# Mixture-of-experts kernel: 684 inner columns as five chunks of 128 and one shared remainder chunk

## The chip, the cores and the metric

The kernel runs on one core of a Trainium2 chip. Its time is the device time of one execution in microseconds (us). Three timed runs of the kernel before took 1914.9, 1920.45 and 1924.0 us; the median, 1920.45 us, is the time before. A profiled execution of its own took 1901.8 us; everything below that speaks of rows, waits and positions in time comes from that one execution.

The engines are named as the profile names them: PE is TensorE's matmul side and PEld its weight loading, DVE is VectorE, ACT is ScalarE, POOL is GpSimd and SP is SyncE, which here only issues DMAs.

## What is computed

The input is four sequences of 1024 tokens with 256 channels, all in float32. The layer is a transformer block with sandwich norms: attention with 16 heads of 16, then a mixture of eight experts of which each token uses two.

```python
def _moe_forward(x, centroid, Wg, bg, W1, b1, W2, b2):   # E = 8, K = 2, D = 256, H = 684
    ...
    w, sel = jax.lax.top_k(dist, K)          # the two farthest centroids
    w = jax.nn.softmax(w.astype(jnp.float32), axis=1).astype(x.dtype)
    ...
    for e in range(E):
        h = jax.nn.silu(xs @ Wg[e] + bg[e]) * (xs @ W1[e] + b1[e])
        out = out + we[:, e:e + 1] * (h @ W2[e] + b2[e])
    return out.reshape(x.shape)

x = x + _layernorm(_L0_attn_ref(_layernorm(x), ...))
x = x + _layernorm(_L0_ffn_ref(_layernorm(x), ...))
```

H = 684 is the number of inner columns of an expert. It is 6 x 114, and also 5 x 128 + 44.

## The kernel before

The kernel has three parts, one after the other on PE.

**Opening and attention, to about 1168 us.** The order of the instructions on PE, DVE and ACT is written out ahead by a planner. The function `step` emits the fixed work (scores `sc`, weighted values `av`, maxima `pm`), and between these it calls `run_one`, which takes the first piece of background work that fits. Background work is a generator wrapped in `Work`; before each of its pieces it yields the engines and nanoseconds that the piece is expected to take, such as `"P500 D400"`. The planner keeps a clock of its own from these numbers. A piece that starts on PE is let in when the planner's clock has passed the end of the piece before it; what a DMA takes is not in that clock unless the generator yields it as `W`. `late_constants` is one such generator. It is made with `Work(late_constants(), 40)`, where 40 is the step by which it is due and not a step before which it may not run. Each engine then executes its own instructions strictly in the order in which they were emitted.

SP's order is not written by hand in this part. SP issues, in this order: the loads that attention starts with; then 34 DMAs that write the tile `empty` over the whole DRAM buffer `rows` (the place where tokens are later scattered by expert); and the DMAs that lay the experts' weights and biases out in the DRAM buffer `wall`, one row of 128 partitions by `WW` floats for each expert. The first `wall` DMA comes ahead of the `rows` DMAs, all others behind them. On this queue at most eight DMAs are in flight: each waits for the one that was issued eight before it.

**The experts, about 1168 to 1829 us.** Tokens are sorted by expert into tiles of `TS` = 256 rows; there are `MT` = 39 tiles. A small table, computed on DVE from the counts per expert, gives each tile its expert and first row (`tabi`). For tile j, `fetch(j)` loads the tokens (`xt`) and the weights of the expert (`w`); `transposed` puts the tokens' channels on partitions (`px`, `xT`); `up` computes the inner columns, and `down` multiplies them by W2 and scatters the weighted rows into `res` with an indirect DMA on POOL. `up` works on chunks of `FP` = 114 inner columns, `NF` = 6 of them, each with four matmuls (two projections, two halves of the 256 channels). ACT takes silu of the gate projection out of PSUM (`sil`), DVE multiplies it by the other projection (`h`). `down` takes the six chunks for each half of the tile's tokens, i = 0 and 1; the last of the six has 115 rows, as a row of ones carries the bias b2. The order on SP, PE, DVE and ACT is written by hand: while tile j goes up, tile j - 1 goes down, and the tokens of tile j + 1 are transposed ahead of the last two chunks.

**The end, from 1829 us.** Results are gathered, normalised and stored. The change does not touch this part.

The line numbers are those of the profile. Lines that matter below: L191 `late_constants`; L226 the `rows` DMAs; L236 to L246 the `wall` DMAs; L1042 to L1069 the table; L1076 `fetch`; L1099 the transposes; L1114 the up-matmuls; L1133 the down-matmuls; L1159 the loads of `x` from `resid` that ACT issues at the start of the experts.

Of the kernel before, what the change touches and what calls it, by code (L numbers as in the profile page):

```python
# [8 lines left out]
F32 = mybir.dt.float32  # L9
# [30 lines left out]
O1, O2, OG, WW = KC * FF, 2 * KC * FF, 2 * KC * FF + NF * C, 2 * KC * FF + NF * C + 2 * NF  # L40
# [3 lines left out]
def sandwich(  # L44
# [168 lines left out]


# [18 lines left out]
    wall = tc.dram_tile([NE, P, WW], F32, name="wall")  # L233
    for e in range(NE):
        for i, w in enumerate((wg, w1)):
            nc.sync.dma_start(  # L236
                out=wall[e, :, i * O1 : (i + 1) * O1].rearrange("p (k f) -> p k f", k=KC),
                in_=w[e].rearrange("(k p) f -> p k f", p=P),
            )
        nc.sync.dma_start(  # L240
            out=wall[e, :FP, O2:OG].rearrange("p (f c) -> p f c", f=NF),
            in_=w2[e].rearrange("(f p) c -> p f c", p=FP),
        )
        nc.sync.dma_start(out=wall[e, FP : FP + 1, OG - C : OG], in_=b2[e : e + 1, :])
    for i, bias in enumerate((bg, b1)):
        nc.sync.dma_start(  # L246
            out=wall[:, :FP, OG + i * NF : OG + (i + 1) * NF].rearrange("e p f -> p e f"), in_=bias
        )
# [353 lines left out]
    def outputs(u, av):  # L602
# [32 lines left out]
        if g == NG - 1:  # L635
# [5 lines left out]
                after=[back] + [closing[k] for k in closing] + before_[:-1],  # L641
# [350 lines left out]
    with tc.manual_schedule(engines={ET.PE, ET.DVE, ET.Activation}):  # L992
# [17 lines left out]
        Work(late_constants(), 40)  # L1010
# [26 lines left out]

    pc = bank("counts")
    nc.tensor.matmul(pc[:, :NE], ones, seen, start=True, stop=True)
    one = slice(0, 1)  # L1040
    cnt = const.tile([1, NE], I32, tag="cnt", name="cnt")
    nc.vector.tensor_scalar(cnt, pc[one, :NE], float(TS - 1), None, ALU.add)  # L1042
    nc.vector.tensor_scalar(cnt, cnt, TS.bit_length() - 1, None, ALU.arith_shift_right)
    num = const.tile([1, NE], F32, tag="num", name="num")
    nc.vector.tensor_copy(num, cnt)
    tri = const.tile([1, NE, NE], F32, tag="tri", name="tri")
    nc.vector.tensor_tensor(
        tri, num[:, None, :].to_broadcast([1, NE, NE]), before[one], ALU.mult
    )
    first = const.tile([1, NE], F32, tag="first", name="first")  # L1050
    nc.vector.tensor_reduce(first, tri, AX.X, ALU.add)
    sh = [1, MT, NE]
# [20 lines left out]
    for h in hs:  # L1073
        nc.gpsimd.memset(h[96:P, NF - 1, :], 1.0)
# [116 lines left out]
    with tc.manual_schedule(engines={ET.SP, ET.PE, ET.DVE, ET.Activation}):  # L1191
        ready, last = [fetch(0), fetch(1)], None
        xT = transposed(0, ready[0][0])
        for j in range(MT):
            xt, w = ready.pop(0)
            up(j, w, xT, 0)
            for i in range(2):
                if last is not None:
                    down(*last, i)
# [95 lines left out]
```

## Time and profile before

| | before |
|---|---|
| median of three timed runs | 1920.45 us |
| profiled execution | 1901.8 us |
| its span, first to last instruction | 1900.0 us |
| PE busy | 1699.6 us (89%) |
| PE busy, 1220 to 1829 us | 608.6 of 609.0 us |
| DVE busy, whole span | 1067.6 us (56%) |
| mean granted PE clock | 0.946 |
| DMA traffic | 197 MB |

The page of a profile shows the span in 40 slices of 47.5 us each; a digit is the busy share in tenths, and 9 is 90% or more. `PEclk` is the clock that TensorE was granted, in tenths of full speed. In a row of instructions, `pu<-xT,w` means that the tile `pu` is written from `xT` and `w`; `128*114` is the shape that the weights take in the array and `128x256` that of the data that is streamed past them. In a timeline the first number is the start in us, the second the length of the merged piece, and `x32` the number of records in it. A line ends with the idle time of the engine just before, and with what ended it, where there was any. SPq and ACTq are the issuing of DMAs by these engines, and not the transfers.

### The profile page before, as it was taken

To read this page: it belongs to the slowest core of one execution; us is meant where nothing else is said; L and a number is where in the kernel's file an instruction comes from. 1 tells how busy PE (TensorE), PEld (TensorE's weight loads), DVE (VectorE), ACT (ScalarE), POOL (GpSimd) and SP (SyncE) were. 2 spreads that over 40 slices of the span, in tenths; PEclk is the share of its full clock that TensorE was granted. 3 is DMA by queue.
4 is the path that set the end of the run, shared out by engine and by line. 5 is a ranking of instruction groups with operands and counts; after the bars stand their busy time and mean duration, and the time that the engine had idled before them with its cause. 6 is when DMAs were issued, how large, how long until landed. Compare 5 with 4: busy or idle time off the path is not lost. (4 is left out here: it accounts for less than half of the span.)

```text
span 1900.0 us, 27442 instructions
## 1 busy us (share of the span) xinstructions
PE 1699.6 (89%) x9640; PEld 1068.7 (56%) x9640; DVE 1067.6 (56%) x2522; ACT 880.6 (46%) x1766; POOL 572.7 (30%) x1068
## 2 busy tenths in 40 slices
PE   4989999999999999999999992799999999999940
PEld 3444445544444454445444441688888888888840
DVE  6576687686677687676678844133333333333346
ACT  2357676776776676676575671111111111111113
POOL 5652422543471544542432132011111111111104
PEclk8899999999999999999999995799999999999975
DMA  8997500100000001000000001844444444444434
GB/s 251 301 299 207 142 1 12 34 34 12 23 1 23 24 34 34 1 12 23 1 35 18 29 31 36 274 167 163 165 162 163 163 164 167 163 164 166 167 125 155
DMA packets 101036, 196.99 MB, mean 104 GB/s; under 512 B 8094, under 2 KB 80437, under 8 KB 95907
## 3 DMA queue, kind: packets, MB, share of 16 engines
q1 hardware_dynamic: 83410, 160.65, 26.1%
q0 software_dynamic: 9040, 26.21, 4.1%
q10 hardware_dynamic: 8448, 8.39, 1.4%
q8 instruction: 76, 1.25, 0.3%
q14 instruction: 62, 0.50, 0.1%
HBM read 132.22 MB, written 79.86 MB: 112 GB/s over the span
## 5 line engine op out<-in xcount | busy, mean ns | idle before, releaser
L594 DVE TENSOR_REDUCE part<-pm 128x1 f32<-128x512 f32 x1024 | 647.6, 684 | 212.3 <-PE pm L590 209.2
L682 ACT ACTIVATE e<-sc 128x512 f32<-128x512 f32 x1024 | 538.2, 603 | 199.1 <-PE sc L678 191.4
L1114 PE MATMUL pu<-xT,w 128*114 128x256 f32 x1872 | 422.3, 383 | 7.4 <-DMA x<-resid 4.6
L1114 PEld LDWEIGHTS pu<-xT,w 128*114 128x114 f32 x1872 | 334.1, 180 | 77.1 <-issue 5.0
L1119 ACT ACTIVATE sil<-pu,w 114x256 f32<-114x256 f32 x234 | 110.3, 474 | 504.3 <-PE pu L1114 495.4
L1122 DVE SCALAR_TENSOR_TENSOR h<-pu,w,sil 114x256 f32<-114x256 f32 x234 | 112.9, 484 | 337.1 <-ACT sil L1119 337.0
L590 PE MATMUL pm<-stack,stack 64*128 64x512 f32 x960 | 267.9, 472 | 20.3 <-DVE part L594 15.5
L740 PE MATMUL av<-e,v 128*32 128x512 f32 x2048 | 281.7, 622 | 0.0
L1146 POOL DMA_INDIRECT res<-yo,ids x78 | 74.8, 959 | 567.8 <-DVE yo L1145 562.7
L671 PE MATMUL sc<-stack,stack 64*128 64x512 f32 x960 | 238.9, 439 | 1.3 <-ACT oT L766 0.7
L678 PE MATMUL sc<-shift,bring 64*128 64x512 f32 x1024 | 235.3, 407 | 3.7 <-ACT shift L579 3.5
L590 PEld LDWEIGHTS pm<-stack,stack 64*128 64x128 f32 x960 | 120.0, 188 | 200.8 <-DVE part L594 118.2
L1133 PE MATMUL pe<-w,h 114*128 114x256 f32 x936 | 214.9, 379 | 0.0
L1133 PEld LDWEIGHTS pe<-w,h 114*128 114x128 f32 x936 | 178.1, 190 | 25.1
L671 PEld LDWEIGHTS sc<-stack,stack 64*128 64x128 f32 x960 | 114.9, 187 | 64.1 <-issue 23.2
L678 PEld LDWEIGHTS sc<-shift,bring 64*128 64x128 f32 x1024 | 120.6, 190 | 25.8 <-ACT shift L579 14.2
L1145 DVE TENSOR_SCALAR yo<-pe,xt 128x256 f32<-128x256 f32 x78 | 37.7, 483 | 104.4 <-PE pe L1133 104.4
L538 ACT CAST stack<-ps 128x512 fp32r<-128x512 f32 x124 | 73.5, 595 | 49.3 <-PE ps L531 48.9
L531 PEld LDWEIGHTS ps<-ident_r,split 128*128 128x128 f32 x512 | 52.2, 144 | 64.3 <-POOL split L262 22.0
L531 PE MATMUL ps<-ident_r,split 128*128 128x128 f32 x512 | 69.4, 264 | 16.0 <-POOL split L262 15.9
L740 PEld LDWEIGHTS av<-e,v 128*32 128x32 f32 x2048 | 41.2, 109 | 72.6 <-issue 66.3
L929 POOL DMA_INDIRECT rows<-xr,to x64 | 62.7, 980 | 62.3 <-DVE to L924 44.7
(246 smaller groups left out, 1432.6 us busy)
## 6 DMA issues: line engine op xcount, KB each, us to landing
w<-wall SPq DMA_DIRECT2D x39, 1368.0 KB, 6.7
rows<-empty SPq DMA_DIRECT2D x34, 1032.0 KB, 15.5
w<-wall SPq DMA_DIRECT2D x39, 689.3 KB
wall<-in_w_dram SPq DMA_DIRECT2D x16, 684.0 KB
xt<-rows SPq DMA_DIRECT2D x39, 258.0 KB
wall<-in_wg_dram SPq DMA_DIRECT2D x8, 684.0 KB
xb<-in_x_dram POOLq DMA_DIRECT2D x8, 512.0 KB, 4.3
resid<-xb SPq DMA_DIRECT2D x8, 512.0 KB, 3.8
```

The lines of the kernel that those rows point to most:

```text
L531: nc.tensor.transpose(ps[:, t * P : (t + 1) * P], splits[b, g, half][:, t, is_k, 2 * pr : 2 * pr + 2].rearrange("p h n d -> p (h n d)"), i ...
L590: nc.tensor.matmul(pm, q[r, t * P : (t + 1) * P], k_[r, half * TB : (half + 1) * TB], start=True, stop=True,)
L594: nc.vector.tensor_reduce(part[:, i, 2 * pr + s, half : half + 1], pm, AX.X, ALU.max)
L671: nc.tensor.matmul(sc, k_[r, kb * P : (kb + 1) * P], q[r, qb * TB : (qb + 1) * TB], start=True, stop=False,)
L678: nc.tensor.matmul(scs[s], bring[pr][r, :], shift[u][r, :], start=False, stop=True)
L682: nc.scalar.activation(e, scs[s], AF.Exp, scale=1.0 / HD**0.5)
L740: nc.tensor.matmul(av[32 * j : 32 * j + 32, :], v_aug[kb][:, 4 * g + j, :], es[j], start=(kb == 0), stop=(kb == NT - 1),)
L1114: nc.tensor.matmul(pu[:FP, i, :], w[:, c0 : c0 + FP], xT[:, k, :], start=(k == 0), stop=(k == KC - 1),)
L1119: nc.scalar.activation(sil, pu[:FP, 0, :], AF.Silu, bias=w[:FP, OG + f : OG + f + 1])
L1122: nc.vector.scalar_tensor_tensor(h[:FP, f, :], pu[:FP, 1, :], w[:FP, OG + NF + f : OG + NF + f + 1], sil, ALU.add, ALU.mult,)
L1133: nc.tensor.matmul(po[:, :C], h[:n, f, i * P : (i + 1) * P], w[:n, O2 + f * C : O2 + (f + 1) * C], start=(f == 0), stop=(f == NF - 1),)
L1146: sent = nc.gpsimd.indirect_dma_start(out=res[:, :], out_offset=bass.IndirectOffsetOnAxis(ap=ids, axis=0), in_=y, in_offset=None,)
```

## The change

The inner columns are cut into `NC` = 5 chunks of 128 and a remainder of `FR` = 44. The remainder columns of both projections stand in one stationary tile of 108 columns: the gate's 44 columns in columns 0 to 43, and the last 64 columns of W1, of which the last 44 are the remainder, in columns 44 to 107, so that the two results land on PSUM partitions 0 to 43 and 64 to 107. One pair of matmuls (the two halves of the channels) so serves both projections. DVE writes the product for the first 128 tokens into rows 0 to 43 of a tile `hr`, and for the second 128 into rows 64 to 107; rows 44 and 108 are ones, for b2. The remainder of W2 is kept twice in `w`, in rows 0 to 44 and 64 to 108, and `down` opens with two matmuls of 45 rows each, one in either row group, before the five full chunks of each half.

Five things come with it. The weights of an expert are written into `wall` by 11 DMAs (88 in all) in place of 4 and two bias DMAs for all. The biases, which come from the host in groups of 114, are brought into groups of 128 on the chip: `late_constants` gets two further pieces, with a way out to DRAM (`lin`) and back (`lined`) between two sets of PE transposes. The closing work of a block waits for `late_constants`. The table of tiles is computed by a function, in tiles that take their place from space that attention leaves. And the order within a tile is now: the remainder chunk, chunks 0 and 1, the first half down, chunks 2 and 3, the second half down, fetch and transposes, chunk 4.

```diff
-O1, O2, OG, WW = KC * FF, 2 * KC * FF, 2 * KC * FF + NF * C, 2 * KC * FF + NF * C + 2 * NF
+NC = FF // P
+FR = FF - NC * P
+R2 = 64
+WK = 2 * FF + (P - R2) - FR
+O2, OB = KC * WK, KC * WK + NC * C
+OR = OB + 2 * (NC + 1)
+WW = OR + C
...
+        yield "P200 A400"
+        pc = bank("plin", pssc)
+        n = NE * NF
+        for i in range(2):
+            nc.tensor.transpose(pc[:n, i * FP : (i + 1) * FP], natural[:, i, :], ident[:FP, :FP])
+        flat = ap1.tile([n, 2, FP], F32, tag="eq", name="flat")
+        nc.scalar.copy(flat, pc[:n, : 2 * FP].rearrange("p (i f) -> p i f", i=2))
+        for i in range(2):
+            nc.sync.dma_start(
+                out=lin[i].rearrange("e (f p) -> (e f) p", p=FP), in_=flat[:, i, :]
+            )
+        lined = ap1.tile([2 * NE, FF], F32, tag="oT", name="lined")
+        nc.sync.dma_start(out=lined, in_=lin.rearrange("i e f -> (i e) f"))
+        yield "P900 A400"
+        pc = bank("pbias_", pssc).rearrange("p (f i) -> p f i", i=2 * NE)
+        for f in range(NC + 1):
+            m = P if f < NC else FR
+            nc.tensor.transpose(
+                pc[:m, f, :], lined[:, f * P : f * P + m], ident[: 2 * NE, : 2 * NE]
+            )
+        biases = ap1.tile([P, NE, 2, NC + 1], F32, tag="gt", name="biases")
+        pool.memset(biases, 0.0)
+        for f in (slice(0, NC), slice(NC, NC + 1)):
+            m = P if f.start < NC else FR
+            nc.scalar.copy(
+                biases[:m, :, :, f].rearrange("p e i f -> p i e f"),
+                pc[:m, f, :].rearrange("p f (i e) -> p i e f", i=2),
+            )
+        nc.sync.dma_start(
+            out=wall[:, :, OB:OR].rearrange("e p w -> p e w"),
+            in_=biases.rearrange("p e i f -> p e (i f)"),
+        )
...
+    lin = tc.dram_tile([2, NE, FF], F32, name="lin")
+    natural = ap1.tile([FP, 2, NE * NF], F32, tag="gt", name="natural")
+    for i, bias in enumerate((bg, b1)):
+        nc.sync.dma_start(out=natural[:, i, :], in_=bias.rearrange("p e f -> p (e f)"))
     for e in range(NE):
-        for i, w in enumerate((wg, w1)):
-            nc.sync.dma_start(
-                out=wall[e, :, i * O1 : (i + 1) * O1].rearrange("p (k f) -> p k f", k=KC),
-                in_=w[e].rearrange("(k p) f -> p k f", p=P),
-            )
+        for w, to, cols in (
+            (wg, 0, slice(0, FF)), (w1, FF, slice(FF - (P - R2), FF)), (w1, FF + P - R2, slice(0, NC * P))
+        ):
+            n = cols.stop - cols.start
+            for k in range(KC):
+                nc.sync.dma_start(
+                    out=wall[e, :, k * WK + to : k * WK + to + n], in_=w[e, k * P : (k + 1) * P, cols]
+                )
         nc.sync.dma_start(
-            out=wall[e, :FP, O2:OG].rearrange("p (f c) -> p f c", f=NF),
-            in_=w2[e].rearrange("(f p) c -> p f c", p=FP),
-        )
-        nc.sync.dma_start(out=wall[e, FP : FP + 1, OG - C : OG], in_=b2[e : e + 1, :])
-    for i, bias in enumerate((bg, b1)):
-        nc.sync.dma_start(
-            out=wall[:, :FP, OG + i * NF : OG + (i + 1) * NF].rearrange("e p f -> p e f"), in_=bias
-        )
+            out=wall[e, :, O2:OB].rearrange("p (f c) -> p f c", f=NC),
+            in_=w2[e, : NC * P].rearrange("(f p) c -> p f c", p=P),
+        )
+        for r in (0, R2):
+            nc.sync.dma_start(out=wall[e, r : r + FR, OR:], in_=w2[e, NC * P :])
+            nc.sync.dma_start(out=wall[e, r + FR : r + FR + 1, OR:], in_=b2[e : e + 1, :])
...
-                after=[back] + [closing[k] for k in closing] + before_[:-1],
+                after=[back, late] + [closing[k] for k in closing] + before_[:-1],
...
-        Work(late_constants(), 40)
+        late = Work(late_constants(), 40)
...
+    tab = hp.tile([1, 2, MT], F32, tag="tab", name="tab")
...
+    hs = [hp.tile([P, NC, TS], F32, tag=f"h{i}", name=f"h{i}") for i in range(2)]
+    hr = [hp.tile([P, P], F32, tag=f"hr{i}", name=f"hr{i}") for i in range(2)]
+    for h in hr:
+        for r in (0, R2):
+            nc.gpsimd.memset(h[r + 32 : r + 64, :], 1.0)
...
         w = wpool.tile([P, WW], F32, tag="w", name=f"w_{j}")
-        for rows_, cols in ((P, slice(0, O2)), (FP, slice(O2, WW))):
+        for p, cols in (
+            (slice(0, P), slice(0, OR)), (slice(0, FR + 1), slice(OR, WW)),
+            (slice(R2, R2 + FR + 1), slice(OR, WW)),
+        )[: n + 1]:
             nc.sync.dma_start(
-                out=w[:rows_, cols],
-                in_=wall[bass.ds(e, 1), :rows_, cols].rearrange("e p w -> (e p) w"),
-            )
-        nc.sync.dma_start(
-            out=w[FP : FP + 1, OG - C : OG],
-            in_=wall[bass.ds(e, 1), FP : FP + 1, OG - C : OG].rearrange("e p w -> (e p) w"),
-        )
+                out=w[p, cols], in_=wall[bass.ds(e, 1), p, cols].rearrange("e p w -> (e p) w")
+            )
...
-    def up(j, w, xT, f2):
-
+    def up(j, w, xT, f):
+
+
+        n = tiles[j] * P
         h = hs[j % 2]
-        for f in (2 * f2, 2 * f2 + 1):
-            pu = psu.tile([P, 2, TS], F32, tag="pu", name=f"pu_{j}_{f}")
-            for i in range(2):
-                for k in range(KC):
-                    c0 = i * O1 + k * FF + f * FP
-                    nc.tensor.matmul(
-                        pu[:FP, i, :], w[:, c0 : c0 + FP], xT[:, k, :],
-                        start=(k == 0), stop=(k == KC - 1),
-                    )
-            sil = sp.tile([FP, TS], F32, tag="sil", name=f"sil_{j}_{f}")
-            nc.scalar.activation(
-                sil, pu[:FP, 0, :], AF.Silu, bias=w[:FP, OG + f : OG + f + 1]
-            )
+        pu = psu.tile([P, 2, TS], F32, tag="pu", name=f"pu_{j}_{f}")
+        m = P if f < NC else R2 + FR
+        for i in range(2 if f < NC else 1):
+            for k in range(KC):
+                c0 = k * WK + (i * (FF + P - R2) + f * P)
+                nc.tensor.matmul(
+                    pu[:m, i, :n], w[:, c0 : c0 + m], xT[:, k, :n],
+                    start=(k == 0), stop=(k == KC - 1),
+                )
+        m = P if f < NC else FR
+        sil = sp.tile([P, TS], F32, tag="sil", name=f"sil_{j}_{f}")
+        nc.scalar.activation(
+            sil[:m, :n], pu[:m, 0, :n], AF.Silu, bias=w[:m, OB + f : OB + f + 1]
+        )
+        bias = w[:m, OB + NC + 1 + f : OB + NC + 2 + f]
+        if f < NC:
             nc.vector.scalar_tensor_tensor(
-                h[:FP, f, :], pu[:FP, 1, :], w[:FP, OG + NF + f : OG + NF + f + 1], sil,
-                ALU.add, ALU.mult,
-            )
-
-    def down(j, xt, w, i):
-
-        h = hs[j % 2]
-        po = bank(f"pe_{j}_{i}")
-        for f in range(NF):
-            n = FP + (f == NF - 1)
-            nc.tensor.matmul(
-                po[:, :C], h[:n, f, i * P : (i + 1) * P], w[:n, O2 + f * C : O2 + (f + 1) * C],
-                start=(f == 0), stop=(f == NF - 1),
-            )
...
+                h[:, f, :n], pu[:, 1, :n], bias, sil[:, :n], ALU.add, ALU.mult
+            )
+        else:
+            for i in range(tiles[j]):
+                c = slice(i * P, (i + 1) * P)
+                nc.vector.scalar_tensor_tensor(
+                    hr[j % 2][i * R2 : i * R2 + FR, :], pu[R2 : R2 + FR, 0, c], bias, sil[:FR, c],
+                    ALU.add, ALU.mult,
+                )
+
+    def down(j, xt, w):
+
+        pos = [bank(f"pe_{j}_{i}") for i in range(tiles[j])]
+        for i, po in enumerate(pos):
+            r = slice(i * R2, i * R2 + FR + 1)
+            nc.tensor.matmul(po[:, :C], hr[j % 2][r, :], w[r, OR:], start=True, stop=False)
+        for i, po in enumerate(pos):
+            for f in range(NC):
+                nc.tensor.matmul(
+                    po[:, :C], hs[j % 2][:, f, i * P : (i + 1) * P],
+                    w[:, O2 + f * C : O2 + (f + 1) * C], start=False, stop=(f == NC - 1),
+                )
...
+            yield
...
-        ready, last = [fetch(0), fetch(1)], None
+        ready, last = [fetch(0), fetch(1)], iter(())
         xT = transposed(0, ready[0][0])
         for j in range(MT):
             xt, w = ready.pop(0)
-            up(j, w, xT, 0)
-            for i in range(2):
-                if last is not None:
-                    down(*last, i)
-                if i == 1:
-                    if j + 2 < MT:
-                        ready.append(fetch(j + 2))
-                    if j + 1 < MT:
-                        nxt = transposed(j + 1, ready[0][0])
-                up(j, w, xT, i + 1)
-            xT, last = nxt, (j, xt, w)
-        for i in range(2):
-            down(*last, i)
+            for f in (NC, 0, 1):
+                up(j, w, xT, f)
+            next(last, None)
+            for f in (2, 3):
+                up(j, w, xT, f)
+            for _ in last:
+                pass
+            if j + 2 < MT:
+                ready.append(fetch(j + 2))
+            if j + 1 < MT:
+                nxt = transposed(j + 1, ready[0][0])
+            up(j, w, xT, 4)
+            xT, last = nxt, down(j, xt, w)
+        for _ in last:
+            pass
```

## The prediction

> **What bounds the kernel now.** I read the page's first two parts, then the busy time by stage, then the instructions in order of time in three places: inside one expert tile, where TensorE (PE) changes its tiling, and at 90 to 100 us, where the change puts new work. Last came SyncE's (SP's) DMA queue of the first 240 us.
>
> ```profile
> span 1900.0 us, 27442 instructions
> PE 1699.6 (89%) x9640; PEld 1068.7 (56%) x9640; DVE 1067.6 (56%) x2522; ACT 880.6 (46%) x1766; POOL 572.7 (30%) x1068
> ...
> PE   4989999999999999999999992799999999999940
> ...
> DMA  8997500100000001000000001844444444444434
> ```
>
> PE is the bound in both long stages; the hole in PE's row at slices 24 and 25 separates attention from the experts. DMA is full only in the first 240 us. By stage (columns: busy us of PE, PEld, DVE, ACT, POOL, then granted clock, DMA share, GB/s):
>
> ```profile
> 95.00:240.00 145.00, 138.11 (x858) 65.76 (x859) 98.95 (x184) 97.31 (x187) 61.93 (x110) 0.98 0.76 212
> 1168.00:1220.00 52.00, 21.88 (x77) 16.27 (x77) 9.49 (x46) 3.91 (x8) 8.35 (x10) 0.62 0.67 206
> 1220.00:1829.00 609.00, 608.58 (x2891) 514.72 (x2890) 188.77 (x499) 107.89 (x228) 73.82 (x77) 1.00 0.44 160
> ```
>
> From 1220 to 1829 us PE is busy 608.6 of 609: what leaves PE there shortens the kernel by its own length. From 95 to 240 it works 138 of 145 us beside a full DMA queue: what stops PE there lengthens the kernel by the length of the stop. One expert tile on PE:
>
> ```profile
> 1292.62 7.07 PE L1114 MATMUL pu<-xT,w 128*114 128x256 f32 x32
> 1299.53 2.76 PE L1133 MATMUL pe<-w,h 114*128 114x256 f32 x12
> 1302.13 3.62 PE L1114 MATMUL pu<-xT,w 128*114 128x256 f32 x16
> 1305.58 2.76 PE L1133 MATMUL pe<-w,h 114*128 114x256 f32 x12
> 1308.17 0.60 PE L1099 MATMUL px<-ident,xt 128*128 128x128 f32 x4
> ```
>
> A float32 matmul is two records. Start to start 32 records take 6.91 us, 12 take 2.60: 0.216 us a record, for 114 columns or 114 rows alike. A tile has 48 + 24 records and a transpose group of 0.44 us: 72 x 0.216 + 0.44 = 15.99 us, 39 times.
>
> **Fewer up-matmuls.** Six chunks of two projections become five, plus one matmul pair over k that holds both remainders: 44 records, not 48. 4 x 0.216 = 0.864 us a tile, x39 = 33.7 us gained. Wider weights (128 columns, not 114) I cost at nothing: the down-matmuls load 128 columns already and run at the same 0.216.
>
> **The paired down-products.** The two 45-row products of a tile (four records, 0.864 us when alone) now stand in rows 0 to 63 and 64 to 127, so they may run side by side: two slots, 0.432 us. But the array changes its tiling before and after them. That is where the Trainium skill speaks against the change: "TensorEngine Tiling (Array Packing)", Tiling Modes, says that changing the mode, not merely the tile, drains the engine. The attention stage shows its price:
>
> ```profile
> 602.66 0.40 PE L671 MATMUL sc<-stack,stack 64*128 64x512 f32 x2
> 602.89 0.40 PE L678 MATMUL sc<-shift,bring 64*128 64x512 f32 x2
> 603.22 1.13 PE L469 MATMUL pv<-wv,nT 128*128 128x256 f32 x4
> 604.28 0.50 PE L671 MATMUL sc<-stack,stack 64*128 64x512 f32 x2
> 604.61 0.40 PE L678 MATMUL sc<-shift,bring 64*128 64x512 f32 x2
> ```
>
> Within one mode the step from sc to sc is 0.23 us; across the change to pv it is 0.33, and the first step after a change is 0.33 again (604.28 to 604.61). pv's four records need 0.864 and take 1.06. So a change costs 0.10 before and 0.10 after, 0.40 for going there and back. Pair: 0.432 + 0.40 = 0.83 against 0.864, a gain of 0.03 a tile. The same skill's "TensorE: Matmul & The Clock Gate", Part 3, has row tiles start 4 ns apart at no other price; by that rule alone the pair would gain 0.43 a tile, 17 us in all. I take the row. That float32 row tiles interleave (both first records, then both second) no row shows; the nearest, av in four column tiles, does eight 512-column records in 0.99 us (601.33 to 602.32), so it interleaves. If row tiles don't, the pair takes three or four slots: 1.05 or 1.26 us, a loss of 0.19 or 0.40 a tile. Experts in sum: 39 x (0.864 + 0.03) = 35 us gained; ends 18 (four slots) and 51 (no price for the mode).
>
> **Other work in a tile.** VectorE (DVE) gets five products of 0.48 us and two of half width instead of six; it is busy 189 of 609 us. After the transposes only 8 records (1.73 us) stand before the next xT is needed, not 16 (3.46): yo (0.48) and the xT copy (0.69) end about 0.9 us after the transposes stop issuing, so 0.8 us of cover is left. If it went, each us late would cost 39. Bytes per fetch rise from 2.06 to 2.17 MB with DMA at 44%: hidden.
>
> **The new bias path.** late_constants now also transposes the two biases on PE, copies them on ACT, sends them to DRAM (lin), loads them back (lined) and transposes again. I looked at where the build puts this. PE's order: pbo, av, ps, pm 4_1_1, then plin (waits for natural's second load), sc, ps, pm 5_0_0, then pbias_ (waits for lined). PE runs in order, so whatever these two wait for stops attention. They stand here in before's time:
>
> ```profile
> 92.75 0.50 PE L590 MATMUL pm<-stack,stack 64*128 64x512 f32 x2
> ...
> 94.00 0.52 PE L590 MATMUL pm<-stack,stack 64*128 64x512 f32 x2
> ```
>
> plin would come at 93.3 us, pbias_ at 94.5. SP's order in the build: natural's first load, the 34 stores of empty into rows, natural's second load, all 88 stores into wall, then lin twice, then lined. SP at that time, before:
>
> ```profile
> 16.60 117.78 SPq L226 DMA_DIRECT2D rows<-empty  x34
> 134.43 3.37 SPq L236 DMA_DIRECT2D wall<-in_w_dram  x1
> ...
> 147.86 8.07 SPq L244 DMA_DIRECT2D wall<-in_b_dram  x1
> ...
> 221.50 6.18 SPq L246 DMA_DIRECT2D wall<-in_b_dram  x1
> ```
>
> The rows stores hold SP until 134.4, and a small DMA behind them lands some 16 us after its issue (the page gives 15.5 for rows; 16.1 in the first 260 us for wall<-in_b_dram). So natural's second half lands near 151: PE waits 93.3 to 151. Then it does some 1.2 us of work and waits for lined, behind all of wall.
>
> How long does wall take? An expert takes 10.7 us (the b2 issues lie 10.7 us apart), 151 + 8 x 10.7 = 237. By that row lin would start at 237. The Trainium skill, "DMA: Bandwidth & Descriptors", in the part on why a DMA increments its semaphore by 16, says a DMA spreads over the largest number of engines up to 16 that divides its outer size: w2's 114 rows go to 6 engines, its new 128 rows to 16. The trace agrees that engines stand idle with the queue never empty (152 to 237 us):
>
> ```profile
> q1 hardware_dynamic: 10306, 13.67, 56.8%
> ```
>
> Spread evenly an expert is 10.7 x 0.568 = 6.1 us. With 3% more bytes, 11 DMAs in place of 4, and only eight in flight (in the build each SP DMA waits for the one eight before it, as it did), I take 7.8: wall ends at 151 + 62 = 213, lin 2.5 us later, lined another 3 (xt lands in 2.4 to 2.8): 219. Ends: 7 us an expert, 212; the old 10.7, 242. PE stands from 94.5 to 219 in place of none: 124.5 us lost (ends 117 and 148). The cover would be other PE work, and there is none: PE is in order and nearly full afterwards. The transposes for plin and pbias_ (16 records, at most 1.8 us by px's 0.11 each), four mode changes (0.8) and the low clock after each of two long idles add 6 us: after the idle before the experts 32 up-records took 9.2 us, not 6.9, so 2.3 us after the second stop and about half that in the 1.2 us of work between the two. POOL's memset of biases waits for plin, with split_2_0 queued behind it; both are done long before 219, so nobody else is late. closing now also waits for late: done by then, nothing.
>
> **Start of the experts.** The table's tiles moved to space that attention leaves, so in the build its 15 DVE operations wait for the last indirect stores (landed near 1187; before, the table was done at 1172.6, amid settle). They take some 4 us, so the first fetch leaves near 1192.5, not 1187.2. Against that ACT sat in the issue of x<-resid until 1207.9 and held up the first sil, so most of those 5 us were lost anyway. I take 3 (ends 0 and 8).
>
> **Sum.** +124.5 + 6 + 3 - 35 = +98.5. The profiled execution took 1901.8 us (span 1900.0 and 1.8 around it), so 2000.3; the median of the three timed runs is 1920.45, 1% above it, and 1920.45 + 98.5 = 2019.
>
> **The rivals.**
> 1. The other side: the biases are no wait. If lined were back by 120.5 us (94.5 + the 26 us that 35 - 3 - 6 pay for) the kernel would break even; with no wait, and so no low clock, it would end at 1920.45 - 35 + 3 + 2.6 = 1891. For it: they are small, and the work is called late. Against it: lined stands behind 122 DMAs on one queue, whose rows part alone lasts to 134 us.
> 2. wall runs at its old rate, 10.7 us an expert, since eight DMAs in flight are now smaller: lined at 242, +23, 2042.
> 3. The row tiles don't interleave: four slots, -18 in place of -35: 2036. This is also the case that the change doesn't do what it says.
> 4. Only natural's wait counts (lined is quick): PE stops to 151, 57 not 124.5: 1951. The order on SP speaks against it.
>
> **How the numbers follow.** Likeliest, as summed: 0.55, 2019, by itself 2002 to 2036 (7 us on the stop, 8 on the experts, 4 on the start, 0.25% between runs). Rival 2: 0.20; rival 3: 0.17; rival 4: 0.04; rival 1: 0.04. The range takes in rivals 2 and 3 and the lower ends: 1992 to 2047. About 0.5% is what a measurement of this kernel can tell from no change; faster by more only in rival 1: 0.04; within it 0.01; slower 0.95.
>
> **What would show it.** In the changed profile PE should be idle in slices 2 to 4, with two waits, plin on natural to about 151 us and pbias_ on lined to about 219, the second in the chain that ended last. An expert tile should be 15.1 us (14.9 if the mode were free, 15.3 to 15.5 if the pair runs in three or four slots), and the pair's records should start together. I am wrong in the main if PE is busy between 100 and 200 us.

## The result, and the profile after

The changed kernel takes 2014.8 us (median of four runs, 2014.1 to 2019.1); the kernel before, run beside it, took 1920.0 us (median of four). The ratio is 1.050, with an interval of 1.048 to 1.052: the change makes the kernel 94.7 us slower. The forecast was 2019 us, within 1992 to 2047.

Part of the page of the changed kernel; the slices are now 50.3 us each:

```profile
span 2013.0 us, 27278 instructions
PE 1667.2 (83%) x9492; PEld 1034.9 (51%) x9492; DVE 1079.9 (54%) x2562; ACT 882.3 (44%) x1769; POOL 572.9 (28%) x1071
...
PE   4600599999899999989999989629999999999950
PEclk8855799999899999999999989859999999999985
DMA  9998200001000000010000010154544544544534
```

PE has 32 us less work than before (1667.2 against 1699.6 us), and the kernel is 95 us longer. PE's row shows where: counted from 0, slices 2 and 3 are empty and 1 and 4 are partly so, where before all four were nearly full. The rest of the row looks as it did, and the granted clock falls to 0.5 in the same place. By stage (columns as in the prediction):

```profile
95.00:250.00 155.00, 31.69 (x176) 15.17 (x176) 18.22 (x30) 19.68 (x39) 30.98 (x49) 0.57 0.73 197
...
1340.00:1940.00 600.00, 590.04 (x2803) 496.29 (x2804) 201.39 (x545) 111.86 (x235) 72.86 (x76) 0.99 0.49 179
```

Between 95 and 250 us PE works 31.7 of 155 us; DVE, ACT and POOL stand with it, and only the DMA queue goes on (0.73 of it busy). What PE waits for there, from the waits of 60 to 300 us (total us, times, longest):

```profile
DVE part L641 <- PE pm L637: 170.4, 28, 77.4
...
PE pbias__950 L240 <- DMA lined<-lin: 73.6, 1, 73.6
...
POOL biases L309 <- PE plin L227: 62.2, 1, 62.2
...
PE plin L227 <- DMA natural<-in_b_dram: 52.1, 1, 52.1
```

Two single waits of PE, 52.1 and 73.6 us, make 125.7 us. The long waits of DVE and POOL are consequences: both wait for PE. In PE's timeline the two stops and what stands between and behind them:

```profile
141.18 0.39 PE L227 MATMUL plin<-ident,natural 114*48 114x114 f32 x1 [52.06 <-DMA natural<-in_b_dram]
141.49 0.79 PE L718 MATMUL sc<-stack,stack 64*128 64x512 f32 x2
...
217.69 0.72 PE L240 MATMUL pbias__950<-ident,lined 16*128 16x16 f32 x6 [73.57 <-DMA lined<-lin]
...
220.17 1.94 PE L787 MATMUL av<-e,v 128*32 128x512 f32 x8
...
224.08 1.07 PE L787 MATMUL av<-e,v 128*32 128x512 f32 x8
```

`av` takes 1.94 us just behind the second stop and 1.07 us four microseconds later: TensorE was granted a clock of 0.50 from 217.6 to 222.5 us and of 0.99 in the 9.5 us after that. The reason for the second stop stands in SP's queue:

```profile
16.30 113.27 SPq L268 DMA_DIRECT2D rows<-empty  x34
129.62 2.06 SPq L279 DMA_DIRECT2D natural<-in_b_dram  x1
131.72 1.94 SPq L286 DMA_DIRECT2D wall<-in_wg_dram  x2
...
154.00 1.23 SPq L286 DMA_DIRECT2D wall<-in_wg_dram  x2
...
163.51 1.23 SPq L286 DMA_DIRECT2D wall<-in_wg_dram  x2
...
211.43 0.98 SPq L231 DMA_DIRECT2D lin<-flat  x2
215.77 0.30 SPq L235 DMA_DIRECT2D lined<-lin  x1
```

`flat` was ready soon after 141 us, but `lin` is issued at 211.4, behind all the stores of the weights into `wall`; here one expert's stores follow the last one's after 9.5 us.

The gain is there too. One expert tile on PE:

```profile
1503.57 0.70 PE L1213 MATMUL pe<-w,hr 45*128 45x256 f32 x4
1504.20 2.42 PE L1216 MATMUL pe<-w,h 128*128 128x256 f32 x10
1506.46 3.62 PE L1186 MATMUL pu<-xT,w 128*128 128x256 f32 x16
1509.92 2.32 PE L1216 MATMUL pe<-w,h 128*128 128x256 f32 x10
1512.08 0.60 PE L1169 MATMUL px<-ident,xt 128*128 128x128 f32 x4
1512.51 6.21 PE L1186 MATMUL pu<-xT,w 128*128 128x256 f32 x28
1518.65 0.70 PE L1213 MATMUL pe<-w,hr 45*128 45x256 f32 x4
```

From pair to pair it is 15.08 us, where a tile before took 15.99. From the first to the last down-matmul the experts take 573.2 us instead of 608.6: 35.4 us gained.

### The profile page after: what moved, and what is told of

The parts are those of the page before. It is cut to its first block, busy times and chain, and to the rows that moved or that the text cites. A ratio compares the mean times of both kernels' runs of the same rounds, so it can differ in the third digit from the quotient of the medians.

```text
span 2013.0 us, 27278 instructions
## 1 busy us (share of the span) xinstructions
PE 1667.2 (83%) x9492; PEld 1034.9 (51%) x9492; DVE 1079.9 (54%) x2562; ACT 882.3 (44%) x1769; POOL 572.9 (28%) x1071
## 5 line engine op out<-in xcount | busy, mean ns | idle before, releaser
L1186 PE MATMUL pu<-xT,w 128*128 128x256 f32 (+1 forms) x1716 | 385.6, 381 | 4.1 <-DMA x<-resid 4.1
L1186 PEld LDWEIGHTS pu<-xT,w 128*128 128x128 f32 (+1 forms) x1716 | 322.0, 189 | 50.2 <-issue 4.5
L1192 ACT ACTIVATE sil<-pu,w 128x256 f32<-128x256 f32 (+1 forms) x234 | 110.6, 473 | 474.1 <-PE pu L1186 474.1
L1197 DVE SCALAR_TENSOR_TENSOR h<-pu,w,sil 128x256 f32<-128x256 f32 x195 | 94.4, 484 | 265.4 <-ACT sil L1192 265.4
L1216 PE MATMUL pe<-w,h 128*128 128x256 f32 x780 | 185.0, 384 | 0.0
L1216 PEld LDWEIGHTS pe<-w,h 128*128 128x128 f32 x780 | 145.0, 190 | 31.1 <-issue 12.9
```

The lines of the kernel that those rows point to most:

```text
L1186: nc.tensor.matmul(pu[:m, i, :n], w[:, c0 : c0 + m], xT[:, k, :n], start=(k == 0), stop=(k == KC - 1),)
L1192: nc.scalar.activation(sil[:m, :n], pu[:m, 0, :n], AF.Silu, bias=w[:m, OB + f : OB + f + 1])
L1197: nc.vector.scalar_tensor_tensor(h[:, f, :n], pu[:, 1, :n], bias, sil[:, :n], ALU.add, ALU.mult)
L1216: nc.tensor.matmul(po[:, :C], hs[j % 2][:, f, i * P : (i + 1) * P], w[:, O2 + f * C : O2 + (f + 1) * C], start=False, stop=(f == NC - 1),)
```

## The experiments

Theory: the loss is PE standing behind two DMAs of the new bias path, whose end is set by the length of SP's queue ahead of `lined`; the rest of the change gains some 32 us. Rivals: the paired products or the larger wall cost something as well; each of the two waits costs its own length; the way through DRAM is slow in itself.

The chips differ: on some the kernel before takes about 1920 us, on others 1888 to 1894. So each time is set beside the kernel before on its own chip. Expectations that name a time mean a chip where the changed kernel takes 2014 us.

**The bias path later.** The last two pieces of `late_constants` become a background work of their own, which may begin only at step 40, and which tells the planner that a DMA of 8 us lies between the two (`W8000`).

```diff
+    def regrouped():
         yield "P200 A400"
...
         nc.sync.dma_start(out=lined, in_=lin.rearrange("i e f -> (i e) f"))
+        yield "W8000"
         yield "P900 A400"
...
-        late = Work(late_constants(), 40)
+        Work(late_constants(), 40)
+        late = Work(regrouped(), 48, start=40)
```

> The changed kernel with the two bias pieces in a generator of their own that may not start before step 40 (near 260 us, when SP's queue is empty), and with 8 us of planner time between them. Theory (PE's two waits are the loss): both waits vanish, 52 + 74 us and the low clock after them; 2015 - 126 - 4 = 1885, faster than before by some 35 us, with the expert tile still at 15.08 us. Rival (the loss comes from 88 wall DMAs in place of 42, or from the changed order in attention): it stays near 2000.

1861.7 us, against 1893.8 for the kernel before: ratio 0.983 (0.981 to 0.985). `plin` now comes when its data has long been there. The view of that tile, and the longest of PE's waits from 60 to 300 us:

```profile
L229 PE MATMUL plin<-ident,natural x2: 261/271/281, 247.5 to 247.6; 114*48 114x114 f32 x2
```

```profile
PE pmx L625 <- DVE mx L621: 5.8, 3, 2.5
```

So neither of the two waits is left, and 5.0% slower becomes 1.7% faster, with the same `wall`, the same experts and the same DMAs. All of the loss lies in the place where PE reaches the two transposes.

**The same beside two variants, on a chip where before takes 1920.5 us.** First the version of the last paragraph once more, then the same with the paired products replaced by two products of 109 rows in the ordinary mode (the rows that belong to the other half of the tokens are zero, and so is the gap between the two copies of W2's remainder, which now come in one fetch), then the same with the table's tiles in space of their own, and the kernel before with a profile.

> The same kernel as e1, as the base for the other two of this series: 0.983 of the kernel before, as in the first series.

1886.1 us, ratio 0.982 (0.980 to 0.984).

```diff
-    hr = [hp.tile([P, P], F32, tag=f"hr{i}", name=f"hr{i}") for i in range(2)]
+    hr = [hp.tile([P, 2, P], F32, tag=f"hr{i}", name=f"hr{i}") for i in range(2)]
...
-            r = slice(i * R2, i * R2 + FR + 1)
-            nc.tensor.matmul(po[:, :C], hr[j % 2][r, :], w[r, OR:], start=True, stop=False)
+            r = slice(0, R2 + FR + 1)
+            nc.tensor.matmul(po[:, :C], hr[j % 2][r, i, :], w[r, OR:], start=True, stop=False)
```

> e1 with the two remainder down-products in one tiling mode: each is a matmul of 109 rows of which the rows of the other half are zeros (hr twice as large, W2's gap of rows zeroed in wall, one fetch of 109 rows in place of two of 45). The products are the same. By the prediction's sum the pair costs 0.83 us a tile side by side, mode changes included, and 0.864 in one mode: 39 x 0.03 = 1 us slower than e1, so no difference that can be seen. By the rule without the price of the mode it would be 39 x 0.43 = 17 us slower.

1893.0 us, ratio 0.986 (0.983 to 0.988). The pair in this kernel's timeline:

```profile
1411.48 1.03 PE L1218 MATMUL pe<-w,hr 109*128 109x256 f32 x4
```

From it to the ten records behind it 0.86 us pass, four slots of 0.216. The experts take 574.8 us in place of 573.2, so the row groups are worth 1.6 us in the whole kernel: 0.04 us a tile, where the prediction had 0.03. The time was expected to move by 1 us and moved by 6.9. The other 5 us between the two medians do not lie in the experts: the two profiles, 3.1 us apart, have 1.7 of it in attention, and where the rest comes from stays open. They are small beside the 17 us that row tiles without a price for the mode would have brought.

```diff
-    tab = hp.tile([1, 2, MT], F32, tag="tab", name="tab")
+    tab = const.tile([1, 2, MT], F32, tag="tab", name="tab")
```

(and so for the table's other tiles; `lined` takes its space elsewhere, tag `xr`)

> e1 with the table's tiles in space of their own, so that DVE can compute it amid the last settle, as in the kernel before; lined moves to a larger tile to make room. The prediction gave the later table 3 us (0 to 8). The traces of before and e1 have the first down-matmul equally long after the end of attention, 76.5 and 76.4 us, as ACT is held by its loads of x. If that is right the time stays that of e1 within 1 us; by the prediction it falls by 3.

1884.0 us, ratio 0.982 (0.979 to 0.984). The stretch from the last copy of attention's output (`ou`) to the first down-matmul is 82.0 us, against 85.8 in the kernel beside it: 3.8 us, where the prediction had 3. The medians lie 2.1 us apart and their intervals overlap, so this gain is seen in the profile and not established by the times.

> The kernel before once more, for its profile. In the profile of the changed kernel attention drifts by a further 24 us after the two waits, in steps of 1 to 5 us, which e2 and e5 don't show. If before can show such steps too (its timed runs took 1915 to 1924 us on one chip and 1891 to 1896 on another), they are the chip's and not the change's.

1920.9 us, span 1919.1. Its attention ends 23 us later than in the profiled execution of before that the prediction read (1901.8 us), by steps of 1 to 5 us spread over the whole of attention. The profiles of the changed kernel and of the variants on this chip show the same steps and those of other chips don't. So these steps go with the chip and are no part of the change (what makes them stays open); it is why a balance needs the two profiles from like chips.

**The first wait away.** The loads of the biases move to the head of SP's queue; everything else is the changed kernel.

```diff
+    natural = ap1.tile([FP, 2, NE * NF], F32, tag="gt", name="natural")
+    for i, bias in enumerate((bg, b1)):
+        nc.sync.dma_start(out=natural[:, i, :], in_=bias.rearrange("p e f -> p (e f)"))
...
-    natural = ap1.tile([FP, 2, NE * NF], F32, tag="gt", name="natural")
-    for i, bias in enumerate((bg, b1)):
-        nc.sync.dma_start(out=natural[:, i, :], in_=bias.rearrange("p e f -> p (e f)"))
```

> The changed kernel with both loads of natural ahead of everything that is slow on SP's queue, and nothing else moved. Theory (the two waits have one end, the landing of lined behind wall): plin no longer waits, but pbias_ waits from about 90 to 217, so the sum of the waits is the same 126 us and the time the same, 2013 to 2015. Rival (each wait is a cost of its own): 52 us faster, 1963.

1981.1 us, ratio 1.046 (1.044 to 1.048). As the changed kernel had run on another chip, both were run again side by side, where before takes 1893.2 us:

> The changed kernel once more, unaltered, so that the two kernels beside it stand against it on one chip. Expected: near 2014, as the first time: two waits, plin on natural of about 52 us and pbias_ on lined of about 74 us, together 120 to 130.

> The changed kernel with the two loads of the biases issued at the head of SP's queue, so that plin finds natural already there. Theory (both waits end at one point, when lined lands behind wall's stores): PE's first wait disappears and the second grows by as much; against the changed kernel of the same chip the time moves by less than 6 us, up or down. Rival (each wait costs its own length): 52 us less than the changed kernel.

The changed kernel took 1981.4 us (ratio 1.047, 1.045 to 1.050), the one with the early loads 1979.4 (ratio 1.047, 1.044 to 1.050): no difference. The 2014 us expected of the changed kernel were those of another chip, and its two waits, 117.2 us, fell just short of the 120 to 130. The waits of the changed kernel on this chip, and then those of the kernel with the early loads:

```profile
PE pbias__950 L240 <- DMA lined<-lin: 71.3, 1, 71.3
...
PE plin L227 <- DMA natural<-in_b_dram: 45.9, 1, 45.9
```

```profile
PE pbias__950 L243 <- DMA lined<-lin: 116.5, 1, 116.5
```

The first wait is gone and the second has grown by 45.2 us, as long as the first was (45.9). Waits in a row with one end are not added up: who takes the first away gains nothing.

**The second wait away.** The stores into `wall` are emitted behind `lined`. On SP's queue most of them then stand behind it; of the first expert's, three still go ahead of `lin` and three between `lin` and `lined`. The bytes, the pieces and the DMAs are the same.

```diff
+    def lay_out_wall():
...
         nc.sync.dma_start(out=lined, in_=lin.rearrange("i e f -> (i e) f"))
+        lay_out_wall()
         yield "P900 A400"
...
-    for e in range(NE):
...
```

> The changed kernel with the stores into wall emitted behind lined, so that in the order of SP's queue most of them (all but a few small ones and two large ones of the first expert) stand behind lin and lined instead of ahead of them. The same bytes, the same pieces and the same DMAs. Theory (the length of the second wait is the queue ahead of lined, not its own way through DRAM): plin still waits for natural to about 141 us, the second wait falls from 74 to 10 to 20 us, and the kernel takes 1950 to 1962. Rival (the way PE, ACT, DRAM and back is itself slow, or the stores behind it now hold up something later, the first fetch of the experts for one): above 1990.

1912.5 us, ratio 1.012 (1.009 to 1.014), on the same chip as the last two: 68.9 us less than the changed kernel. SP's queue and PE's two stops:

```profile
122.90 2.04 SPq L298 DMA_DIRECT2D natural<-in_b_dram  x1
...
133.64 0.80 SPq L249 DMA_DIRECT2D lin<-flat  x2
...
136.46 0.46 SPq L253 DMA_DIRECT2D lined<-lin  x1
...
206.78 0.51 SPq L270 DMA_DIRECT2D wall<-biases  x1
```

```profile
132.85 0.39 PE L245 MATMUL plin<-ident,natural 114*48 114x114 f32 x1 [39.41 <-DMA natural<-in_b_dram]
...
140.09 0.72 PE L259 MATMUL pbias__950<-ident,lined 16*128 16x16 f32 x6 [4.30 <-DMA lined<-lin]
```

The whole way PE, ACT, DRAM, back and PE takes 7.2 us (132.85 to 140.09), of which PE waits for 4.3. `wall` is done no sooner (the last DMA into it is issued at 206.8 us), and nothing is seen to suffer from it. The wait fell further than the 10 to 20 us expected, and the time by 5 us more than the 52 to 64 us that the range meant. The theory holds: the second wait was the queue ahead of `lined`, not the way. Of the 19.3 us that are left over before, the two waits that remain (43.7 us) and the later start (3), less the 35.4 of the experts, give 11.3; set beside the profile of the later bias path, this one is 3.7 us later over the two stops than they are long, and the last 4 are not accounted for.

**The bias path alone.** The kernel before, with the two new pieces and their DMAs added, and the closing work made to wait for them; what they compute goes to a DRAM tile that nobody reads, and the experts use the old layout.

```diff
+        yield "P200 A400"
+        pc = bank("plin", pssc)
...
+        nc.sync.dma_start(
+            out=scrap[:, :, :].rearrange("e p w -> p e w"),
+            in_=biases.rearrange("p e i f -> p e (i f)"),
+        )
...
+    scrap = tc.dram_tile([NE, P, 2 * (NC + 1)], F32, name="scrap")
```

> The kernel before with the bias path alone added (two loads of natural, plin, lin, lined, pbias_, and a store of the biases to a scratch buffer that nothing reads); experts, wall and table are those of before. Theory: nearly the whole loss appears, PE waiting from about 89 us until lined lands behind the old wall DMAs. If those are bound by w2's 114 rows, 10.7 us an expert, lined lands near 141 + 86 + 6 = 233 and the time is 1920 + 145 + 4 = 2069; if wall took as long as in the changed kernel, lined would land near 218 and the time be 2050. Rival (the loss belongs to the new experts or to wall's 88 DMAs): within 10 us of 1920.

2028.2 us, ratio 1.071 (1.069 to 1.073): 134.4 us over the kernel before. Its waits:

```profile
PE pbias__897 L231 <- DMA lined<-lin: 84.4, 1, 84.4
...
PE plin L218 <- DMA natural<-in_b_dram: 44.0, 1, 44.0
```

The two make 128.4 us; 6.0 us remain for the transposes, the mode changes and the low clock, the sum of which the prediction put at 6 (a remainder, and not read from a profile). The loss is less than the 149 us expected for such a rate: `lined` came at 223 and not at 233, since `wall` began at 126.1 us, before `natural` had landed (135.9). The old `wall` runs at 10.5 us an expert between 158.7 and 200.6 us, with the DMA engines 70% busy; the changed kernel's runs at 9.2 to 9.9, 9.6 in the mean, from 154 us on.

**What sets the rate of `wall`.** The prediction had taken 7.8 us an expert. First the halves of the channels in one DMA each, as in the kernel before, so eight stores an expert and not eleven:

```diff
-            for k in range(KC):
-                nc.sync.dma_start(
-                    out=wall[e, :, k * WK + to : k * WK + to + n], in_=w[e, k * P : (k + 1) * P, cols]
-                )
+            nc.sync.dma_start(
+                out=wall[e, :, :O2].rearrange("p (k f) -> p k f", k=KC)[:, :, to : to + n],
+                in_=w[e].rearrange("(k p) f -> p k f", p=P)[:, :, cols],
+            )
```

> The changed kernel with each of the three weight stores of an expert written as one DMA over both halves of the channels, 8 DMAs an expert in place of 11, the same bytes. If wall's 9.6 us an expert are the issuing of 11 DMAs (0.5 to 1.2 us each on SP), it falls to about 7 and lined lands some 20 us earlier: 1995. If wall is bound by the bytes, nothing moves: 2013 to 2015.

1994.2 us, ratio 1.053 (1.051 to 1.055), slower by 13 us than the kernel with the early loads on that chip (1981.1), which takes the changed kernel's time. Neither expectation held. SP's queue shows why:

```profile
142.58 0.62 SPq L285 DMA_DIRECT2D wall<-in_wg_dram  x1
143.25 0.60 SPq L289 DMA_DIRECT2D wall<-in_w_dram  x1
149.29 0.57 SPq L285 DMA_DIRECT2D wall<-in_w_dram  x1
...
154.04 0.61 SPq L285 DMA_DIRECT2D wall<-in_wg_dram  x1
```

SP stands from 143.9 to 149.3. In the build the store of 64 columns there waits for the `wg` store of its own expert, issued at 142.58, and such a store lands 6.7 us after its issue in this kernel: 149.3. With both halves in one DMA the ranges that the two cover in a row of `wall` interleave, and the build orders one behind the other, though no byte is common to them. The waits of SP in this kernel have it eight times, once an expert (total us, times, longest):

```profile
SPq L285 <- DMA wall<-in_wg_dram: 46.6, 8, 9.3
```

So this experiment put in a wait of its own and says nothing on the rate.

The other way: the changed kernel with the four small stores of an expert (W2's remainder twice, b2 twice) on POOL.

```diff
-            nc.sync.dma_start(out=wall[e, r : r + FR, OR:], in_=w2[e, NC * P :])
-            nc.sync.dma_start(out=wall[e, r + FR : r + FR + 1, OR:], in_=b2[e : e + 1, :])
+            nc.gpsimd.dma_start(out=wall[e, r : r + FR, OR:], in_=w2[e, NC * P :])
+            nc.gpsimd.dma_start(out=wall[e, r + FR : r + FR + 1, OR:], in_=b2[e : e + 1, :])
```

> The changed kernel with the four small stores of each expert (W2's remainder twice, b2 twice) issued by POOL at the start of the kernel, so that SP's queue holds seven stores an expert and not eleven, with 4% fewer bytes; the order in the build also brings both loads of the biases ahead of the rows stores. What is read is the distance of one expert's stores from the next on SP's queue, 9.5 to 9.7 us in the changed kernel with the DMA engines 84% busy, of which the issuing alone is 7.4 us (seen where nothing waits). If the small stores held the queue up (they take four of the eight places in flight and 2.8 us of issuing), the distance falls to 8 to 8.4 us with the engines near full. If the engines' own time sets it, it falls by the 4% of the bytes only, to 9.1 to 9.4 us. Either way plin no longer waits and the end of the stop moves by eight times the difference.

One run, 1971.9 us, beside 1887.8 for the kernel before. SP's queue, and the DMA queue's line from 140 to 190 us:

```profile
146.15 1.76 SPq L286 DMA_DIRECT2D wall<-in_wg_dram  x2
...
187.78 1.18 SPq L286 DMA_DIRECT2D wall<-in_wg_dram  x2
```

```profile
q1 hardware_dynamic: 9455, 12.86, 104.8%
```

Five experts in 41.6 us are 8.3 us each, with the engines full; the same line of the changed kernel, from 154 to 202 us, reads

```profile
q1 hardware_dynamic: 8545, 10.93, 83.8%
```

So the engines' own time for the seven large stores is 8.3 us, and with the small ones on the queue an expert takes some 1.2 us more while the engines stand idle for part of it. What holds SP up in the changed kernel, from 131 to 212 us:

```profile
SPq L286 <- DMA wall<-in_w_dram: 15.0, 8, 2.6
```

That is one wait of 1.9 us an expert; nearly all the rest of the 9.6 us is issuing, of which the four small stores take 2.8. In the trace the store that waits (issued at 158.16) waits for the large W2 store eight places ahead of it, whose last part landed at 158.14. So the limit of eight in flight and the issuing both play a part; how the 1.2 us divide between them was not tested.

`plin` came without a wait here, and PE still stood 96.0 us for `lined`. The time gained little: 84.1 us over before, where the changed kernel is 88.2 over on its chip. Attention itself started 16 us later (first `av` at 97.3 us, against 81.6), with PE waiting 25.7 us for POOL's `split` in the first 110 us, where the changed kernel waits 12.6 in the first 90; POOL was issuing the small stores then.

## Why the prediction was right

The forecast was 98.5 us over before. The spans of two profiles on like chips (before at 1920.9 us, the changed kernel at 2014.9) differ by 93.9. Stage by stage, measured at the last copy of attention's output and at the first and the last down-matmul:

| step | predicted | measured |
|---|---|---|
| PE stands for the two DMAs | +124.5 | 52.1 + 73.6 = +125.7 |
| transposes, modes, low clock | +6 | +4.1 over the two stops |
| rest of attention | 0 | -3.7 (1.6 before the stops, 2.1 behind them), so +126.1 in all by its end |
| start of the experts | +3 | +3.0 |
| experts | -35 | -35.4 |
| end | 0 | +0.1 |

The first 1.6 us may be chance: the two profiles of the kernel before have their first `av` at 82.4 and at 85.2 us.

**The experts.** Both terms stood. The pair's price can be read off the tile: `pu`'s 28 records start at 1512.51 and the last of them 27 x 0.216 later, at 1518.34; the pair comes at 1518.65, 0.31 later and not 0.216. From the pair to the next records it is 0.63 (1503.57 to 1504.20), and these ten take 2.26 us to the next group where the other ten take 2.16. So the step is 0.10 longer than a slot four times: into the pair, inside it, out of it, and once in the ten records behind it. The pair costs 0.82 us in all, predicted 0.83. The two first records start 6 to 7 ns apart and the two second ones 320 ns behind, in all 39 tiles: float32 row tiles do interleave, and rival 3 falls. Here the row of attention was the better guide than the 4 ns of the Trainium skill's "TensorE: Matmul & The Clock Gate", Part 3, taken alone; its "TensorEngine Tiling (Array Packing)", Tiling Modes, had named the drain, and this trace gives it a size. The cover for the xT copy held: the up-matmuls waited 4.1 us in the whole kernel, all of it for something else:

```profile
L1186 PE MATMUL pu<-xT,w 128*128 128x256 f32 (+1 forms) x1716 | 385.6, 381 | 4.1 <-DMA x<-resid 4.1
```

**The stop.** Its mechanism and length were right, but two terms of its sum were wrong and cancelled. The prediction let `natural` land at 151 us and let 62 us of `wall` begin then. In fact the `rows` stores were done at 129.6 and not at 134.4, SP had issued `natural` by 131.7 and went on at once with `wall`: with up to eight in flight, a store doesn't wait for the landing of the one just ahead of it. `natural` landed at 141, some 10 us after its issue and not 16 (the 16.1 us read were those of small stores right behind an old W2 store, which itself takes 16 to 19 us to land in that trace), and `wall` began 19 us earlier than forecast. And it took 79.7 us (131.7 to 211.4), 18 us longer: 13.7 for the first expert, 9.4 in the mean for the others, where 7.8 had been taken. Here the step that failed is "Spread evenly an expert is 10.7 x 0.568 = 6.1 us". The share of 56.8% was read over 152 to 237 us, and the last `wall` store of the kernel before is issued at 221.5; SP had nothing more to issue for the rest of that window. From 152 to 210 us the same view of before reads

```profile
q1 hardware_dynamic: 6707, 11.04, 65.6%
```

which gives 10.7 x 0.656 = 7.0 us. And even that is no measure of full engines: with the small stores moved away they were full and an expert still took 8.3 us. With 1.2 us for the small stores that is the 9.5 measured; why full engines need 8.3 where the share of before gives 7.0 isn't shown. As one stop followed the other with no useful work between them, only the end counted: predicted 219, measured 217.7 us, and PE reached the place 4 us sooner than taken (88.8 and not 93.3). So the closeness of 124.5 and 125.7 is luck; what the views of before supported was the range of 212 to 242. One sign that the prediction named can't be read: the profile follows the chain that ended last back to 1324 us only, so it doesn't show the second wait.

The Trainium skill's rule from "DMA: Bandwidth & Descriptors", in the part on why a DMA increments its semaphore by 16, agrees with the traces: in that of before a W2 store of 114 rows lands in six parts, the last 16 to 19 us after its issue; in that of the changed kernel one of 128 rows lands in sixteen, the last after 6.4 to 8.0. The engines are 66% busy from 152 to 210 us in the one and 84% from 154 to 202 us in the other. But the rule only said that the rate of before could be beaten, not by how much.

**The start.** +3.0 us on like chips, and the variant with the table's tiles kept apart gives back 3.8. Against the profiled execution that the prediction read it would be -0.9 (87.1 before, 86.2 after): that execution was long by 4 us in this place, as the other two profiles with the old table have 83.2 and 83.6. The profiles with the new one have 85.6 to 87.1.

**The rivals.** 1 (no wait, 1891 us) is what the later bias path makes real: 1886.1. 2 (`wall` at its old rate, 2042) was not right, though the rate was nearer the old than the one taken; the early start made up for it. 3 falls with the pair's rows. 4 (only `natural`'s wait, 1951) is the kernel with `lined` ahead of `wall`: by estimate 1.0115 x 1920 = 1942 on a chip like the first.

## What to carry to other kernels

When new work is put on an engine that runs in order, ask first what that work waits for, and then what stands ahead of *that* on its queue; here some 126 us hung on a transfer that needs 7.2 us by itself, moving the place of the work cures it (34 us faster than before in place of 95 slower), and moving the DMA in its queue brings back 69 us. A due step alone doesn't keep work from coming too early: give the planner an earliest step, and tell it of a DMA between two pieces. (The run that mended it did both at once; what each does alone was not tried.) Where several waits follow one another with nothing between them, look for the last end: taking the first away moved nothing.

## What the runs showed of the hardware that was not expected

Fewer and larger DMAs were slower (11.0 us an expert in the mean, against 9.2 in the kernel with the early loads on that chip), since an order between stores with interleaved ranges came in with them; the seven stores left when the small ones were moved off ran at 8.3 us with the engines full. A small store costs its issuing and its place on the queue more than its bytes: the four are 4% of the bytes and some 13% of the time. The multiplication into `hr`, for half the width and a third of the partitions, took DVE 353 ns where a full one takes 484; DVE was busy 201 of 600 us in the experts, so this cost nothing. And chips differ: 1888 to 1894 us on some and 1920 on others for the same program, the difference lying in many small steps of attention, nearly as much as all that the good part of this change brings. The lowest median beside its own before is that of the changed kernel with the later bias path and the table's tiles kept apart, 1884.0 us beside 1920.5, not told apart by the times from the later bias path alone.
